# Layer 2 of a four-layer image kernel: its stores issued by Pool instead of SP, and longer transfers assumed in its list schedule

## The chip, the cores and the metric

The kernel runs on one core of one Trainium2 chip. The metric is the device time of one launch in microseconds (us), as the median of three runs; smaller is better.

The engines are called PE (matrix products), DVE (VectorE), ACT (ScalarE), POOL (GpSimd) and SP (SyncE). SP computes nothing here and issues DMAs; POOL can compute and can issue DMAs too.

## What is computed

The input x has 8 images of 32 channels with 256 x 256 pixels, in float32. Four layers follow one another, each of the form x = x + f(group_norm(x)). Layer 0 is two 3x3 convolutions in hyperbolic coordinates with batch norms, layer 1 a Laplace operator in the Fourier domain, layer 3 a local binary pattern. The change concerns layer 2, which mixes within windows of 8 x 8 pixels. Cut to what matters (`b` windows, `c` = 16, `C` = 32, `S` = 2, `WS` = 8):

```python
def _fastkan(x, ln_g, ln_b, ws, wb, bb):
    ln = _layernorm(x, ln_g, ln_b)
    basis = exp(-((ln[..., None] - GRID) / DENOM) ** 2)      # 8 grid points
    return flat(basis) @ ws.T + silu(x) @ wb.T + bb
...
y = _layernorm(wins, pn_g, pn_b)                             # over the 32 channels
a = _fastkan(y regrouped along the columns of a window, k1)  # 16 features
d = _fastkan(y regrouped along the rows of a window, k2)     # 16 features
e = _fastkan(y, k3)                                          # 32 features
z = _fastkan(a + d + e, k4)                                  # 32 features
out = z + wins
```

The result of layer 2 is x3 = x2 + out, where wins is the group norm of x2.

## The kernel before

**Layer 2 in pieces.** `mixing` (L1338) works through one image after another in units of 128 partitions x 2048 pixels (1 MB). Each image has four kinds of jobs, and intermediate results go through DRAM because each kind wants another order of the pixels:

- `image_norm` (8 jobs an image) loads a unit of x2 (tile xt), normalizes it, writes y (tile yt) and silu(y) (tile st), and stores both. The order in DRAM makes each of these two stores eight DMAs of 128 KB (`turned`, L1392).
- `down_columns` (8 jobs) loads y (one DMA) and silu(y) (16 DMAs), applies the first map and stores a (tile ot, one DMA of 1 MB).
- `along_rows` (8 jobs) loads y and silu(y) (two DMAs each), transposes on PE, applies the second map, and stores d (tile ot, two DMAs of 512 KB).
- `third` loads y (four DMAs) and silu(y), a and d (eight DMAs each) and leaves a + d + e in the tile at. `fourth` (8 jobs of each an image) loads x2 again (tile xt), applies the last map, adds, takes the statistics for the next group norm, and stores x3 (tile xt, one DMA of 1 MB).

A map consists of `normed` (L1213, L1237: center, square, norm on PE, ACT and DVE), `front` (L1250: exponents on ACT) and `back` (L1276: products on PE; L1294: exponents on ACT; L1304: the steps from one grid point to the next on DVE). `silu` has L1328 and L1335 on DVE and L1330 on ACT. `evacuate` (L1441) brings the results from PSUM to a tile.

**What sets the order.** Nothing is ordered by hand. Every job adds tasks to a `Plan` (L120 on): an engine, an assumed duration, the buffers it reads and writes, and a `lag`, the time after the engine is free again until the result counts as there. `Plan.issue` runs a list schedule in assumed time: each engine takes the ready task of lowest rank whose buffers are free, and the instructions are written out in the order in which this schedule starts them. On the chip each engine executes its own list strictly in order and waits at semaphores. The assumed times so decide the order, and nothing else.

**The DMAs of layer 2.** All of them are issued by SP, through two helpers: `load` (L1380) plans 0.55 us for each DMA and a lag of LOAD = 10 us; `store` (L1383) plans 0.55 us for each DMA and a lag of STORE = 8 us. In the profile L1381 is any load and L1384 any store. Tiles yt, st and xt have two buffers each, shared by loads and by results that are stored; ot has one buffer (B_OT) for a and d together. A load of y, silu(y), a or d of an image waits until the stores that wrote it have landed.

In the compiled program the DMAs of a queue take eight completion semaphores in turn. A DMA that takes a semaphore waits until the one that had it before, eight DMAs earlier on its queue, has landed.

**What else touches POOL and SP.** Once an image, the statistics of x3 are turned into a group norm (`combine_stats`), whose power of -0.5 is computed by POOL (L240, L241) between two DVE operations (L239, L259). In layer 0 the third pass stores its 64 units from POOL (L810), with 1.0 us and a lag of 16 us planned for each.

Of the kernel before, what the change touches and what calls it, by code (L numbers as in the profile page):

```python
# [1337 lines left out]
def mixing(cx, x2, norms, x3, ydr, sdr, adr, ddr):  # L1338
# [3 lines left out]
    nc = cx.nc  # L1342
    out_norms = cx.stat.tile([P, NB, 2], F32, name="norm3", tag="norm3")
    nc.scalar.preload_act_table_set(LOG_SET)
    with (
# [27 lines left out]
        plan = Plan()  # L1373
# [1 line left out]
        unit = lambda pool, tag, bufs, late=0.0: Buf(pool, [P, UN], tag, bufs, late)  # L1375
        half = lambda h: slice(h * HF, (h + 1) * HF)
        mem = {(n, b): Buf(None, None, None, 0) for n in "ysad" for b in range(NB)}
        LOAD, STORE = 10.0, 8.0

        def load(dmas, reads, bufs):  # L1380
            plan.add("SP", 0.55 * len(dmas), lambda: [nc.sync.dma_start(o(), i) for o, i in dmas], reads, bufs, lag=LOAD)  # L1381

        def store(dmas, bufs, writes):  # L1383
            plan.add("SP", 0.55 * len(dmas), lambda: [nc.sync.dma_start(o, i()) for o, i in dmas], bufs, writes, lag=STORE)  # L1384

        def by_row(dr, k):

# [20 lines left out]
        def image_norm(b, k):  # L1408
            if k == 0:

                scaled[b] = Buf(work, [P, NC], "cs", 2)
                plan.add(
                    "DVE", 0.2,
                    lambda: nc.vector.tensor_scalar(scaled[b][:], center[32][:], norms[:, b, 0:1], None, ALU.mult),
                    [], [scaled[b]],
                )
            xin = x2[b].rearrange("c (rb r) w -> rb c (r w)", rb=4)
            xt = unit(io, "xt", 2)
            load([(lambda: xt[:], xin[:, :, k * UN : (k + 1) * UN])], [], [xt])
            y, sg = unit(io, "yt", 2, L_Y), unit(io, "st", 2, L_Y)  # L1420
            xs = mixer.normed(xt, scaled[b], 32, vecs[:, 2, b : b + 1], mixer.spread)
            plan.add(
                "DVE", 1.25,
                lambda: nc.vector.tensor_scalar(
                    y[:], xs[:].rearrange("p i n -> p (i n)"), pn[:, 0:1], pn[:, 1:2], ALU.mult, ALU.add
                ),
                [xs], [y],
            )
            put = lambda dr, name, t: store(
                [(i, lambda o=o: o(t)) for o, i in turned(dr[b], k)], [t], [(mem[name, b], k)]  # L1430
            )
            put(ydr, "y", y)
            mixer.silu(y, sg)
            put(sdr, "s", sg)
# [10 lines left out]
        def down_columns(b, hf, k):  # L1445
            ch = hf * 16
            at = lambda dr: dr[b][:, ch : ch + 16, k * UN : (k + 1) * UN].rearrange("h c q -> c h q")
            y, sg = unit(io, "yt", 2), unit(io, "st", 2)
            load([(lambda: y[:], at(ydr))], [mem["y", b]], [y])

            dmas = []
            for j in range(4):
                for i in range(4):
                    src = sdr[b][:, ch + 4 * i : ch + 4 * i + 4, k * UN + j * FD : k * UN + (j + 1) * FD]
                    dmas.append(
                        (lambda i=i, j=j: sg[32 * j : 32 * j + 32, i * FD : (i + 1) * FD], src.rearrange("h c q -> c h q"))
                    )
            load(dmas, [mem["s", b]], [sg])
            es = mixer.front(kans[1], y)
            acc = mixer.back(kans[1], es, sg)  # L1460
            out = unit(io, "ot", B_OT)
            evacuate(acc, out, kans[1].bias)
            store([(at(adr), lambda: out[:])], [out], [(mem["a", b], (hf, k))])

        def along_rows(b, k):
# [54 lines left out]
            for g in range(2):  # L1520
                pd = mixer.two(L_D)
                plan.add("PE", 1.2, lambda pd=pd, g=g: turn_back(pd, g), [dc], [pd])
                for c in range(2):
                    for s in range(2):
                        plan.add(
                            "DVE", 0.4, lambda pd=pd, g=g, c=c, s=s: ordered(pd, g, c, s), [pd], [(ot, (g, c, s))]
                        )
            dst = ddr[b].rearrange("h (c s) q -> s (h c) q", s=2)
            store(
                [(dst[s][:, k * n : (k + 1) * n], lambda s=s: ot[:, s, :]) for s in range(2)],  # L1530
                [ot], [(mem["d", b], k)],
# [190 lines left out]
def layers(ctx: ExitStack, tc: tile.TileContext, ins, out):  # L1722
# [26 lines left out]
    x3 = image("x3_", [P, NPIX])  # L1749
    rows = [8, NC, 32 * W]  # L1750
    norms = mixing(cx, x2, norms, x3, *(image(n, rows) for n in ("y_", "s_", "a_", "d_")))

    tc.strict_bb_all_engine_barrier()
# [120 lines left out]
```

## Time and profile before

| | us |
|---|---|
| median of three runs | 14024.65 |
| lowest, highest | 14023.85, 14066.98 |
| the profiled execution, its own time | 14021.73 |
| its span in the profile | 14020.0 |
| busy: PE, DVE, ACT, POOL in the whole span | 10705.7, 8731.4, 7714.0, 166.6 |
| layer 2 within the span | 5715 to 12815 |
| an image of layer 2 in its middle part | 856 to 864 |

The mean granted clock of PE is 0.842 of full speed. The profile is one execution. In its views, "L1276" is a line of the kernel, "acc<-en" says that tile acc is written from tile en, and "SPq" is SP's queue of DMA issues. A line of the waits view reads: engine and line that waited, who ended the wait, then us in total, number of waits, longest. "DMA yt<-y" as the one who ended a wait is a transfer that landed. The DMA queues of the profile are q1 for all that SP issues and q0 for what POOL issues.

### The profile page before, as it was taken

The numbers are of one execution on the slowest core, as the hardware profiler recorded it, in microseconds if no ns is written. First come the engines' busy times: TensorE is split into PE (matmuls) and PEld (weight loads), VectorE is DVE, ScalarE is ACT, GpSimd is POOL, SyncE is SP. The second block draws the span as 40 slices with busy tenths as digits, with TensorE's granted clock in tenths as the row PEclk, the third lists the DMA queues.
The fourth block names the chain that finished last, engine by engine and source line by source line (L and its number), as shares of the span: only waits on it lengthen the run. The fifth ranks groups of instructions, "written<-read, shape, count | busy, mean of one in ns | idle before, by whom it ended". The sixth has DMA issues, their size and how long they took to land.

```text
span 14020.0 us, 359842 instructions
## 1 busy us (share of the span) xinstructions
PE 10705.7 (76%) x165700; PEld 4220.3 (30%) x165700; DVE 8731.4 (62%) x7524; ACT 7714.0 (55%) x6456; POOL 166.6 (1%) x340
## 2 busy tenths in 40 slices
PE   5877899974447899367887878878788788987666
PEld 1222233320016566122332323323232233322222
DVE  3544343344564554256787878878787788887555
ACT  2332444443310222366877778777777778775555
POOL 0000000000000000100000000000000000000000
PEclk8887889975557899588998989989899899998777
DMA  5344333345642244455566556655665565553444
GB/s 95 75 91 91 95 100 103 102 116 187 196 148 77 95 149 149 109 148 144 143 150 155 145 145 150 153 147 137 156 150 151 141 151 147 132 132 98 129 126 126
DMA packets 1562774, 1834.96 MB, mean 131 GB/s; under 512 B 634352, under 2 KB 1279536, under 8 KB 1495728
## 3 DMA queue, kind: packets, MB, share of 16 engines
q1 hardware_dynamic: 1527472, 1744.72, 47.9%
q0 software_dynamic: 33792, 67.21, 1.5%
q8 instruction: 1301, 21.32, 0.6%
q14 instruction: 209, 1.71, 0.0%
HBM read 1140.39 MB, written 671.12 MB: 129 GB/s over the span
## 4 chain that ended last, share of the span: by engine, by line
PE 15%; DVE 14%; DMA 11%; ACT 10%; SPq 5%; issue 4%; DVEq 0%; ACTq 0%; POOL 0%; POOLq 0%
PE acc L1276 10%; DVE en L1304 8%; DMA raw<-x 4%; ACT e L1250 4%; DMA yt<-y 3%; DMA xt<-x 3%; SPq L1381 2%; DVE xc L1237 2%; PE q L1196 2%; SPq L1701 1%; DVE s L1682 1%; ACT e L1294 1%; ACT xc L1213 1%; PE q L1221 1%; SPq L1384 1%
## 5 line engine op out<-in xcount | busy, mean ns | idle before, releaser
L1276 PE MATMUL acc<-en,k_kw 32*32 32x512 f32 x49152 | 2164.5, 626 | 492.1 <-DVE en L1304 454.3
L1304 DVE SCALAR_TENSOR_TENSOR en<-e,en 128x2048 f32<-128x2048 f32 x1024 | 2343.7, 2289 | 210.6 <-PE acc L1276 155.7
L1250 ACT ACTIVATE e<-xc,off 128x2048 f32<-128x2048 f32 x768 | 1515.0, 2008 | 569.2 <-DVE xc L1237 489.2
L1304 DVE SCALAR_TENSOR_TENSOR en<-e 128x2048 f32<-128x2048 f32 x512 | 1170.8, 2287 | 348.4 <-ACT e L1294 190.8
L1276 PEld LDWEIGHTS acc<-en,k_kw 32*32 32x32 f32 x49152 | 710.4, 105 | 1482.9 <-DVE en L1304 1009.7
L1276 PE MATMUL acc<-e,k_kw 32*32 32x512 f32 x16384 | 1036.2, 673 | 104.0 <-ACT e L1294 35.5
L1237 DVE TENSOR_TENSOR xc<-xc,q 128x1024 f32<-128x1024 f32 x640 | 751.0, 1215 | 489.8 <-PE q L1230 489.5
L1294 ACT ACTIVATE e<-e 128x2048 f32<-128x2048 f32 x512 | 970.3, 1924 | 1.5
L1682 DVE TENSOR_TENSOR s<-raw 128x2313 f32<-128x2313 f32 (+2 forms) x256 | 627.7, 2495 | 478.3 <-DMA raw<-x 478.3
L1668 PE MATMUL acc<-s,mats 32*32 32x512 f32 x16384 | 697.9, 728 | 231.9 <-ACT s L1685 223.1
L1685 ACT ACTIVATE s<-s,vecs 128x2313 f32<-128x2313 f32 (+2 forms) x256 | 554.4, 2170 | 553.7 <-DVE s L1682 553.7
L405 ACT ACTIVATE u<-acc,k_vec 128x1024 f32<-128x1024 f32 x256 | 270.8, 1108 | 1062.3 <-DMA v<-u 694.0
L391 PE MATMUL acc<-pad,wb 32*32 32x512 f32 x18432 | 736.9, 649 | 141.1 <-issue 131.8
L1213 ACT ACTIVATE lsq<-q 128x1024 f32<-128x1024 f32 x512 | 526.6, 1028 | 530.6 <-PE q L1196 468.1
L434 DVE TENSOR_TENSOR u<-u,q 128x1024 f32<-128x1024 f32 x256 | 312.4, 1220 | 738.6 <-PE q L429 547.7
L391 PE MATMUL acc<-pad,k_cw 32*32 32x512 f32 x18432 | 736.6, 625 | 15.7 <-ACT u L405 10.8
L711 PE MATMUL n<-sq,k_gather 128*32 128x512 f32 x1024 | 243.7, 1045 | 439.6 <-ACT sq L729 438.2
L1276 PE MATMUL acc<-sg,k_kws 128*32 128x512 f32 x4096 | 504.5, 636 | 47.9 <-DVE sg L1335 40.6
L1196 PE MATMUL q<-yt,k_center 32*32 32x512 f32 x4096 | 313.2, 722 | 284.3 <-DMA yt<-y 227.8
L1213 ACT ACTIVATE xc<-q 128x1024 f32<-128x1024 f32 x512 | 529.3, 1034 | 0.0
L348 PE MATMUL q<-f,k_spread 32*128 32x512 f32 x1024 | 392.8, 853 | 173.2 <-DVE pad L588 93.0
L1071 PE MATMUL po<-ea,us 128*128 128x256 f32 x2048 | 506.5, 391 | 1.2 <-ACT us L1067 1.2
(291 smaller groups left out, 15967.4 us busy)
## 6 DMA issues: line engine op xcount, KB each, us to landing
v<-u SPq DMA_DIRECT2D x512, 256.0 KB
xt<-x SPq DMA_DIRECT2D x128, 1024.0 KB
pad<-v SPq DMA_DIRECT2D x64, 1024.0 KB
v<-v SPq DMA_DIRECT2D x64, 1024.0 KB
xt<-in_x SPq DMA_DIRECT2D x64, 1024.0 KB
x<-xt POOLq DMA_DIRECT2D x64, 1024.0 KB, 38.8
xt<-x SPq DMA_DIRECT2D x32, 2048.0 KB
x<-xt SPq DMA_DIRECT2D x32, 2048.0 KB
```

What stands on the lines that cost most here:

```text
L391: nc.tensor.matmul(acc[i // 2][32 * j : 32 * j + 32, i % 2, :], w[rows, tap, :], pad[rows, r : r + 2, dx : dx + W], start=tap == 0, stop=t ...
L1071: nc.tensor.matmul(po[:, t, :], us[:, c, t:W:2], ex[:, j, c, :], start=c == 0, stop=c == 1)
L1196: nc.tensor.matmul(pc[32 * j : 32 * j + 32, t, :], center[rows, :], src[rows, j * FD : (j + 1) * FD], start=True, stop=True,)
L1213: lambda pc=pc, h=h, fn=fn, out=out: nc.scalar.activation(half(out, h), flat(pc.get()), fn, bias=bias),
L1237: lambda pr=pr, h=h: nc.vector.tensor_tensor(half(xc, h), half(xc, h), flat(pr.get()), ALU.mult),
L1250: nc.scalar.activation(es[d][:], xs[:].rearrange("p i n -> p (i n)"), AF.Exp if exp else AF.Square, bias=kan.off[:, d : d + 1], scale=2.0 ...
L1276: nc.tensor.matmul(acc[bank][32 * to : 32 * to + 32, :], w[rows, out] if w.shape[-1] == P else w[rows, :], rhs[rows, cols] if rhs.shape[-1 ...
L1294: plan.add("ACT", 1.91, lambda: nc.scalar.activation(es[d][:], es[d][:], AF.Exp, scale=-1.0), [], [es[d]])
L1304: lambda: nc.vector.scalar_tensor_tensor(n[:], es[-1][:], BIG, prev[:], ALU.min, ALU.mult),
L1668: nc.tensor.matmul(acc[i][32 * j : 32 * j + 32, :], mats[part, m, part], rhs[part, 2 * j : 2 * j + 2, :], start=m == 0, stop=m == len(weig ...
L1682: nc.vector.tensor_tensor(d, raw[:, r0 + dy : R + 1 + dy, c0 + dx : c1 + dx], raw[:, r0 : R + 1, c0:c1], ALU.subtract)
L1685: nc.scalar.activation(d, d, AF.Sigmoid, scale=vecs[:, 0, b : b + 1])
```

## The change

In `mixing`, the helper `store` plans its task on POOL instead of SP, with 1.0 instead of 0.55 us for each DMA, and issues with `nc.gpsimd.dma_start`. The assumed lags become 12 us for loads and 14 us for stores. Every store of layer 2 goes through this helper: 1280 DMAs. Loads stay on SP with 0.55 us each.

```diff
-        LOAD, STORE = 10.0, 8.0
+        LOAD, STORE = 12.0, 14.0
 
         def load(dmas, reads, bufs):
             plan.add("SP", 0.55 * len(dmas), lambda: [nc.sync.dma_start(o(), i) for o, i in dmas], reads, bufs, lag=LOAD)
 
         def store(dmas, bufs, writes):
-            plan.add("SP", 0.55 * len(dmas), lambda: [nc.sync.dma_start(o, i()) for o, i in dmas], bufs, writes, lag=STORE)
+            plan.add("POOL", 1.0 * len(dmas), lambda: [nc.gpsimd.dma_start(o, i()) for o, i in dmas], bufs, writes, lag=STORE)
```

Since the schedule is computed from these numbers, the order of the instructions of layer 2 changes on all engines, from its first image on. Their number and kind stay the same but for the issuer of the stores. On POOL, the group norm of an image comes behind the last store of x3 of that image.

## The prediction

> **What bounds the kernel now.** I first read the windows view, to place layer 2. It fills 5715 to 12815 us of the 14020.0 us span. After its start-up this is its row (columns: stretch, length, busy time of PE, PE weight load, DVE, ACT, POOL, then granted clock, DMA share, GB/s):
>
> ```profile
> 5945.00:12815.00 6870.00, 5566.01 (x96336) 2034.88 (x96336) 5330.06 (x3674) 5178.19 (x4402) 6.25 (x23) 0.91 0.58 144
> ```
>
> PE is busy 81% of it, DVE 78%, ACT 75%, POOL not at all. No engine is full: the order of the work and the waits at its joints set the pace, and PE stands idle 1304 us. So the next view is who ends PE's waits in that stretch (total us, times, longest):
>
> ```profile
> PE q L1196 <- DMA yt<-y: 192.5, 32, 17.8
> PE q L1196 <- DMA xt<-x: 77.9, 5, 18.4
> PE q L1483 <- DMA yt<-y: 17.5, 2, 14.2
> PE q L1483 <- DMA st<-s: 3.0, 1, 3.0
> ```
>
> Late loads cost PE 290.9 us directly; no compute engine waits there for a store to any amount. The loads come from SP, in order, between the stores. So I read SP's own waits over the layer; L1384 are stores, L1381 loads:
>
> ```profile
> SPq L1381 <- PE q L1196: 806.6, 70, 35.0
> SPq L1384 <- DVE ot L1518: 579.8, 37, 26.5
> SPq L1384 <- DVE xt L1568: 406.2, 47, 38.9
> SPq L1384 <- DMA xt<-x: 223.5, 29, 11.9
> ```
>
> All lines at L1384 add to 1643 us, those at L1381 to 1884 us: for 1643 us SP stands before a store whose data isn't there, or whose completion semaphore is still in use, and each load behind it stands too. The timeline of SP shows how that looks (start, us, queue, line, transfer):
>
> ```profile
> 5746.67 16.66 SPq L1384 DMA_DIRECT2D y<-yt  x8
> 5763.42 0.55 SPq L1381 DMA_DIRECT2D xt<-x  x1
> 5764.07 17.10 SPq L1384 DMA_DIRECT2D s<-st  x8
> 5781.26 5.07 SPq L1384 DMA_DIRECT2D y<-yt  x8
> 5786.43 0.55 SPq L1381 DMA_DIRECT2D xt<-x  x1
> ...
> 8507.54 22.19 SPq L1384 DMA_DIRECT2D y<-yt  x8
> 8529.82 5.79 SPq L1381 DMA_DIRECT2D at<-a  x8
> ```
>
> Eight stores need 5.07 us of issue when nothing holds them, and 16 to 22 us when they stand behind a slow xt load: in the compiled program the DMAs of a queue take eight completion semaphores in turn, so each waits for the eighth before it. In the start-up (one image's norm units, 5715 to 5935 us) the xt loads come 23.6 us apart: (5904.83 - 5763.42) / 6.
>
> The only POOL stores of this kernel stand in layer 0, at L810 (min/median/max; 1 MB each):
>
> ```profile
> L810 POOL DMA_DIRECT2D x<-xt x64: 680/680/887, 3122.7 to 4083.9; - x64
> ...
> DMA to landing us min/median/max: 15.1/38.8/48.4
> ```
>
> **What the Trainium skill says.** "DMA: Bandwidth & Descriptors", section "Issuing engines are not separate DMA queues": transfers from several issuers run on the same 16 engines, and a second issuer saves only sequencer time. That fits what I expect to win, which is SP's time and not bandwidth. The same page, "Queues, rings and completion order": each DMA engine goes round its queues packet by packet, so POOL's stores would no longer stand behind an xt load in one queue. Nothing in layer 2 shows it yet, since only SP's queue carries data there. The same page, "Why a DMA increments its semaphore by 16 and not by 1": a transfer is spread over the largest number up to 16 that divides the slowest dimension of both sides. With 4 row blocks the xt load gets 4 engines; the trace agrees, with a DMA share of 0.25 from 5720 to 5745 us, when only xt loads run. POOL's L810 stores have the same shape, and the last of them ran at a share of 0.25 too (4090 to 4097 us). Layer 2's stores have slowest dimensions of 32, 16 or 128 and would get all 16. "SBUF - State Buffer", "SBUF: two separate sides": a fast-mode DVE operation on one fp32 SBUF source locks POOL out of writing DMA descriptors. Such are L1424 and L1328 (1.34 and 1.22 us against 2.29 us for two sources); no run here shows the lock.
>
> **Part 1: what SP loses.** By medians, SP's stores cost 512 x 0.601 + 512 x 0.598 + 128 x 0.378 + 64 x 0.564 + 64 x 0.344 = 720 us of issue, and 1643 us of waits. SP isn't full, so this is no saving in itself; it is worth what the loads behind gain. Of SP's waits 1643 / (1643 + 1884) = 47% belong to stores; the others wait for a buffer that PE still reads, or for semaphores of other loads, and stay. I take the same share of PE's waits: 0.47 x 291 = -137 us. The ends: 0, if the buffers are what makes these loads late, and -291.
>
> **Part 2: what POOL gains.** POOL issues 1280 DMAs; at L810's 0.68 us that is 870 us in 7100 on an idle engine. It counts only by how long eight stores take from the first issue to the last landing; call it B. The L810 landings are no direct measure, since 1 MB on four engines at the 77 GB/s seen at the end (4090 to 4100 us) takes 13.6 of the 15.1 us, leaving 1.5 us fixed. Eight stores of 128 KB: 5.5 us of issue, or 1 MB at layer 2's 144 GB/s = 7.3 us, whichever is longer, then those 1.5 us: 9 us with nothing in the way. The upper end is 27 us, half way between L810's 15.1 and 38.8, which came with loads in the way. I take 11 us, near the lower end, because a running xt load is in the way on only four of the sixteen engines. The planner now assumes 8 x 1.0 + 14 = 22 us for such a group, so its order leaves room for that. Against this, SP's groups took 5 to 22 us of issue alone, so the buffers yt, st and ot are held no longer than now.
>
> **Part 3: start-up.** A norm unit stores y and s, two groups of eight in series over eight semaphores: 2B = 22 us, beside an xt load (10 to 19 us) and ACT's 10 us. 22 replaces 23.6: 8 x -1.6 = -13 us; ends -46 (17.8 us a unit, the xt load's usual time) and +243 (B = 27).
>
> **Part 4: POOL's other work.** Once an image the group norm (L240, L241) is on POOL and DVE waits for it; it is now behind stores, and behind DVE wait PE and ACT. Today's waits are 5.8 us in 8 times. Each can be between 0.7 and B = 11 us; I take 3: 8 x 3 - 5.8 = +18 us; ends 0 and +82. The DVE lock touches single operations of 1.3 us; I take nothing, since POOL's groups are a few us in an otherwise free 50.
>
> **Part 5: the new delays, 12 and 14 for 10 and 8.** They cost no instruction; they reorder every engine of layer 2. An order with longer loads puts other work before their readers, which is the kind of wait listed above; an order with longer stores delays the users of a buffer. No row prices this. I take 0 and keep 1% of the layer, 70 us, either way as my choice; four steady images lie 856 to 864 us apart, so a worse order would repeat seven times.
>
> **Sum.** -137 - 13 + 18 = -132 us. The profiled execution took 14021.73 us around its span of 14020.0, 2.9 us below the median of 14024.65; so 14024.65 - 132 = 13893 us.
>
> **Rivals.**
> 1. Stores land late (slower). One mechanism: groups of eight on POOL's eight semaphores, each waiting for the last. It decides above B = 23.6 / 2 = 11.8 us: from there the start-up grows by 16 x (B - 11.8), and yt and st, two buffers each, stay taken, so loads come no earlier. With B = 27: +243, and nothing from part 1: 14024.65 + 243 = 14268 us. For it: the median landing of 38.8 us at L810. Against: the shape on four engines. Chance 0.28.
> 2. The change does not reach the bound. The 860 us an image are set by the chain PE to DVE (PE L1276 waits 454.3 us for DVE en L1304), and a load that is earlier only turns into that wait. Parts 3 and 4 remain: 14024.65 - 13 + 18 = 14030 us, no change. Chance 0.15.
> 3. All load waits go, start-up at 17.8 us: 14024.65 - 291 - 46 = 13688 us. For it: loads and SP are 18% of the chain in layer 2. Chance 0.09.
> The forecast, 13780 to 13980 us: 0.48.
>
> **Numbers.** About 0.3%, 42 us, is what a measurement of this kernel can tell from no change. Faster: 0.48 + 0.09 = 0.57; same 0.15; slower 0.28. The range goes from 13730 to 14230 us: it leaves out half of rival 1 and most of rival 3.
>
> **What would show it.** Part 1: L1384 gone from SP's waits, PE's waits for yt and xt near 150 us. Part 2: POOL's L1384 at 0.7 us each, landings near 11 us for a group; over 12 us, with waits of DVE or ACT for y<-yt, s<-st or a<-ot, speak for rival 1. Part 3: xt loads 22 us apart. Part 4: DVE L259 waiting 2 to 4 us an image. Rival 2: the DMA waits shrink, images stay 860 us apart. I am wrong if images come further apart with POOL's stores on time: then the order of part 5 is the cause.

## The result and the profile after

The kernel after takes 13885.28 us in the median (13881.95 to 13906.22), the kernel before in the same series 14024.25 us: a ratio of 0.9898, 95% interval 0.9876 to 0.992. That is 139 us less; 132 had been forecast. The profiled execution of the kernel after, the slowest of its four, has a span of 13904.0 us, which is 116 less than in the profile before, at a mean granted clock of 0.85.

Three instants divide layer 2 in both traces: its first xt load, its first load of y (here the start-up ends), and the group norm at the end of each image.

| us from the first xt load of layer 2 | before | after |
|---|---|---|
| first load of y | 219.7 | 161.7 |
| first group norm | 1749.8 | 1655.8 |
| second to fifth | 2610.5, 3466.5, 4327.2, 5190.8 | 2501.2, 3342.1, 4190.8, 5038.2 |
| last group norm | 7097.4 | 6952.6 |
| where the first xt load stands in the span | 5714.9 | 5740.0 |

The layer is 145 us shorter: 58 of them are gone by the end of the start-up, 87 come later, in images that are 841 to 849 us apart in the middle instead of 856 to 864. Against this the layer begins 25 us later in this profile, though nothing ahead of it was changed; I come back to that at the end.

The windows view of the kernel after from its start-up to its last group norm (columns as in the prediction):

```profile
5900.00:12700.00 6800.00, 5587.54 (x96368) 2045.69 (x96368) 5335.00 (x3686) 5185.51 (x4405) 683.26 (x1192) 0.92 0.57 146
```

PE, DVE and ACT do the work they did before in 70 us less; POOL is busy with 683 us of issue, and the DMA share did not rise. PE's own busy time did not fall (5587.54 us, before 5566.01), so the slightly higher granted clock is not what gained. Who ends PE's waits for loads once the first y has come, from 5945 us on in both traces (to 12700 here, to 12815 in the prediction's list):

```profile
PE q L1196 <- DMA yt<-y: 102.3, 28, 10.0
PE q L1196 <- DMA xt<-x: 26.6, 5, 5.9
PE q L1483 <- DMA yt<-y: 19.7, 1, 19.7
PE acc L1276 <- DMA st<-s: 2.6, 3, 1.7
```

Together 151 us, where it was 291. SP's own waits over layer 2:

```profile
SPq L1381 <- PE q L1196: 1474.0, 84, 37.3
SPq L1381 <- PE acc L1276: 641.9, 83, 31.4
SPq L1381 <- DMA xt<-x: 312.9, 34, 15.4
SPq L1381 <- DMA x<-xt: 308.1, 27, 40.7
SPq L1381 <- PE q L1483: 280.3, 31, 18.2
```

L1384 is gone from SP, as it had to be. But SP is no freer: its waits at L1381 add to 3738 us, where loads and stores together had 1880 + 1546 = 3427 us in nearly the same stretch. SP now stands mostly before loads whose buffer PE still reads (L1196, L1276). The time it no longer spends in front of stores it spends waiting for buffers.

POOL's stores, one line of the kernel, with the work that POOL waited for and those that waited for POOL:

```profile
L1384 POOL DMA_DIRECT2D y<-yt x512: 522/582/1729, 5772.4 to 11308.9; - x171
L1384 POOL DMA_DIRECT2D s<-st x512: 522/607/1307, 5787.1 to 11322.2; - x171
...
  DVE ot L1518: 2299.8, 64
  DVE xt L1568: 1482.8, 66
  ACT ot L1441: 1006.5, 45
...
  ACT st L1330: 27.0, 5
  DVE st L1328: 10.1, 2
  DVE yt L1424: 2.4, 3
...
DMA to landing us min/median/max: 2.6/5.4/13.7
```

An issue of y or s takes 0.58 to 0.61 us, a store lands 5.4 us after its issue began in the median, and compute engines wait for stores 40 us in the whole layer, where it was 130 in the kernel before, nearly all of it in the start-up. POOL itself stands 4.8 ms, by the three lines in the middle, before data that isn't there yet. Nothing is queued behind it, so that costs nothing.

In the start-up the chain of waits shows what paces it now (start, us, what):

```profile
5787.08 7.40 DMA s<-st
5794.52 0.53 issue
5795.05 9.32 DMA y<-yt
5804.41 0.53 issue
5804.94 1.06 POOL s L1384 x2
5806.05 11.05 DMA s<-st
```

A store lands 7.4 to 11.1 us after its issue, mostly about 9.5, and the next one on its semaphore goes. The xt loads are no longer in this chain. The 9.5 us are one turn of a semaphore, from one store to the next that takes it, and not the prediction's B, which runs from the first issue of eight to the last landing. POOL's timeline shows one whole group, the eight y stores from 5795.05 us on, and the s stores that take their semaphores (in brackets: idle before, and who ended it):

```profile
5795.05 0.53 POOL L1384 DMA_DIRECT2D y<-yt  x1 [2.38 <-DMA s<-st]
...
5803.55 0.52 POOL L1384 DMA_DIRECT2D y<-yt  x1 [0.88 <-DMA s<-st]
5804.94 1.64 POOL L1384 DMA_DIRECT2D s<-st  x3 [0.86 <-DMA y<-yt]
...
5813.08 1.31 POOL L1384 DMA_DIRECT2D s<-st  x1 [0.62 <-DMA y<-yt]
```

The eighth s store waits for the eighth y store, which lands shortly before 5813.08: B is 18 us here. But the groups are not in series. The first s goes at 5804.94, as soon as the first y has landed, so the groups follow one another at 9.5 to 10 us. By the updates of the semaphores in the trace, B is 14 to 18 us for the groups of the start-up until the last few, and 10 to 11 us in the median later.

### The profile page after: what moved, and what is told of

Its sections match the earlier page's. It is cut to its first block, busy times and chain, and to the rows that moved or that the text cites. A ratio compares the mean times of both kernels' runs of the same rounds, so it can differ in the third digit from the quotient of the medians.

```text
span 13904.0 us, 360826 instructions
## 1 busy us (share of the span) xinstructions
PE 10721.7 (77%) x165700; PEld 4228.4 (30%) x165700; DVE 8730.9 (63%) x7524; ACT 7715.9 (55%) x6456; POOL 910.6 (7%) x1620
## 4 chain that ended last, share of the span: by engine, by line
PE 14%; DVE 13%; DMA 11%; ACT 9%; issue 8%; SPq 3%; POOL 0%; DVEq 0%; ACTq 0%; POOLq 0%
PE acc L1276 9%; DVE en L1304 7%; DMA raw<-x 4%; ACT e L1250 3%; DMA yt<-y 2%; DVE xc L1237 2%; SPq L1701 1%; PE q L1196 1%; DMA xt<-x 1%; DVE s L1682 1%; ACT st L1330 1%; DMA st<-s 1%; SPq L1381 1%; PE q L1230 1%; PE q L1221 1%
## 5 line engine op out<-in xcount | busy, mean ns | idle before, releaser
L1276 PE MATMUL acc<-en,k_kw 32*32 32x512 f32 x49152 | 2154.8, 620 | 459.6 <-DVE en L1304 428.1
L1276 PEld LDWEIGHTS acc<-en,k_kw 32*32 32x32 f32 x49152 | 713.3, 104 | 1447.5 <-DVE en L1304 961.6
L1276 PE MATMUL acc<-e,k_kw 32*32 32x512 f32 x16384 | 1043.0, 662 | 109.3 <-ACT e L1294 33.7
L391 PE MATMUL acc<-pad,k_cw 32*32 32x512 f32 x18432 | 736.7, 625 | 16.8 <-ACT u L405 11.4
L1276 PE MATMUL acc<-sg,k_kws 128*32 128x512 f32 x4096 | 507.4, 638 | 64.8 <-DVE sg L1335 51.9
L1221 PE MATMUL q<-lsq,k_gather 128*32 128x512 f32 x2560 | 460.8, 658 | 86.4 <-ACT xc L1213 85.7
```

The lines of the kernel that those rows point to most:

```text
L391: nc.tensor.matmul(acc[i // 2][32 * j : 32 * j + 32, i % 2, :], w[rows, tap, :], pad[rows, r : r + 2, dx : dx + W], start=tap == 0, stop=t ...
L1221: nc.tensor.matmul(pn[32 * i : 32 * i + 32, 0, :], gather[:], sq[:, i, :], start=True, stop=True)
L1276: nc.tensor.matmul(acc[bank][32 * to : 32 * to + 32, :], w[rows, out] if w.shape[-1] == P else w[rows, :], rhs[rows, cols] if rhs.shape[-1 ...
```

## The experiments

All ratios are to the kernel before, with 95% intervals. Diffs are against the kernel before unless another is named. The kernels differ in three things that the change made together: who issues the stores, the order of the work, and the lags that lead to that order.

**The queue alone (e1).** The plan stays as it was, so all compute engines keep their order; only the issuer changes.

```diff
-            plan.add("SP", ..., lambda: [nc.sync.dma_start(o, i()) for o, i in dmas], ...)
+            plan.add("SP", ..., lambda: [nc.gpsimd.dma_start(o, i()) for o, i in dmas], ...)
```

> The plan is that of the kernel before (store tasks on SP, 0.55 us for each DMA, lags of 10 and 8 us), so every compute engine keeps the order of before; only the issue of the layer-2 stores goes through Pool. Theory 1 (loads no longer stand behind stores on SP; the new lags are worth nothing): nearly all of the gain, about 13895 us, ratio 0.99; start-up 162 us instead of 220. Theory 2 (the new order is what gains): within 0.3% of before, 14010 to 14040 us.

Measured: 0.9932 (0.9918 to 0.9945), two thirds of the gain. Layer 2 takes 7005.6 us, 92 less: 42 by the end of the start-up (178.2 us, not the 162 expected), 50 later.

**The order alone (e2).** The plan of the kernel after, with POOL as planned engine and lags of 12 and 14, but `nc.sync` in the issue.

> The plan is that of the changed kernel (store tasks on Pool, 1.0 us for each DMA, lags of 12 and 14 us), so every compute engine keeps its order; the stores are issued by SP, in the places where that plan starts them. Theory 1: no gain, or a loss, since the order reckons with loads that do not stand behind stores: 14020 to 14120 us. Theory 2: about 13900 us.

Measured: 0.9979 (0.9968 to 0.9991), between the two theories. The new order is worth 0.2% with all stores still on SP.

**POOL with the old lags (e3).** The kernel after with `LOAD, STORE = 10.0, 8.0`.

> The changed kernel with the old lags of 10 and 8 us; stores are planned and issued on Pool. Theory 1: as the changed kernel within 0.3%, 13850 to 13930 us. Theory 2: near before, 13990 us or more.

Measured: 0.9925 (0.9913 to 0.9938). Of the 1.02% of the change, 0.75% stay without its lags.

**The lags alone (e4).** The kernel before with `LOAD, STORE = 12.0, 14.0`.

> The kernel before with the lags of 12 and 14 us; stores are planned and issued on SP. Theory 1: as before within 0.3%, since SP still holds loads behind stores. Theory 2: a good part of the gain, 13960 us or less.

Measured: 0.9974 (0.9964 to 0.9984). So the queue alone is worth 0.7% and the lags alone about 0.25%, and the two about add up: 0.9932 x 0.9974 = 0.9906, beside 0.9898 (0.9876 to 0.992) measured for both.

**Which lag (e10, e11).** The kernel after with `LOAD, STORE = 12.0, 8.0`, and with `10.0, 14.0`.

> The kernel after with the load lag of 12 and the store lag put back to 8. The kernel after is at 0.9898, and with both lags put back at 0.9925. If the load lag carries the 0.26% (loads placed earlier in SP's queue), this run gives about 0.990; if the store lag carries it (the planner reads y and s back later behind their stores), about 0.9925.

> The kernel after with the store lag of 14 and the load lag put back to 10: the other half of the same question. If the load lag carries the gain, about 0.9925; if the store lag does, about 0.990; if the two only work together, both this run and the one with the load lag alone stay near 0.9925.

Measured: 0.9911 (0.9898 to 0.9925) and 0.9907 (0.9893 to 0.9921). Both lie between the two expected values, and their intervals touch or overlap those of both neighbours. It isn't decided; that each lag carries half fits, and so does noise.

**Which stores (e5, e6).** Only the groups of eight (y and s) on POOL, and then only a, d and x3, with the plan of before. Both are one condition in `store`:

```diff
-            ... [nc.sync.dma_start(o, i()) for o, i in dmas] ...
+            ... [(nc.gpsimd if len(dmas) == 8 else nc.sync).dma_start(o, i()) for o, i in dmas] ...
```

> Order of before on every compute engine. Only the stores of y and silu(y), the groups of eight DMAs, are issued by Pool; a, d and x3 stay on SP. Theory A (what costs is that groups of eight share SP's eight semaphores with slow loads, so the group and all behind it stand): most of the 0.68% that moving all stores gave under this order, ratio 0.994 or less. Theory B (what costs is SP standing before a store whose data is not there, above all ot and xt, 1310 us of SP waits): only the start-up gains its 40 us, ratio 0.997.

> Order of before on every compute engine. Only the stores of a, d and x3 are issued by Pool; y and silu(y) stay on SP in their groups of eight. Theory A: within 0.2% of before, start-up as before (220 us). Theory B: about half a per cent faster, start-up as before.

Measured: 0.9933 (0.992 to 0.9946) for y and s, the whole effect of the queue; 1.0012 (1.0006 to 1.0019) for a, d and x3, a small loss. These are SP's waits for stores in the kernel that keeps y and s on SP:

```profile
SPq L1384 <- DMA xt<-x: 212.7, 23, 13.5
SPq L1384 <- DVE yt L1424: 163.2, 33, 14.9
SPq L1384 <- DMA yt<-y: 70.9, 78, 2.7
```

All its L1384 waits add to 504 us, 1042 less than before, since `DVE ot L1518`, `DVE xt L1568` and `ACT ot L1441` are no longer among them. And the kernel is not faster. A thousand microseconds of SP standing before unfinished results could go without any gain. They moved: SP's waits at L1381 rise from 1880 to 2724 us, most of it before buffers that PE still reads (L1196, L1276 and L1483, 1211 us before, 1911 now), and PE's own waits for loads are no shorter (322 us from 5970 us on, after its first y, where the kernel before had 291). What cost must lie with the y and s stores: their standing behind an xt load, or SP's time to issue 1024 of them, 614 us by the medians. The experiments on the split tell these two apart.

**What an xt load does to the stores behind it** can be read from the trace of the kernel before, at the s stores of 5764.07 us (the timeline is in the prediction). The load ahead of them goes at 5763.42 and lands at 5780.60. SP issues seven stores until 5770; the eighth takes the semaphore of the load and goes at 5780.62. But the seven don't land earlier either. By the updates of their semaphores the first one lands at 5780.84, 16.8 us after its issue, where the y stores from 5781.26 on, with no load ahead of them, take 2.4 us each. While the seven are in flight, the DMA share (last column but one) sinks close to the 0.25 of the load alone:

```profile
5764.00:5769.00 5.00, 1.90 (x10) 0.52 (x8) 0.00 (x0) 4.51 (x4) 0.00 (x0) 0.50 0.87 190
5769.00:5780.00 11.00, 6.65 (x44) 0.83 (x40) 5.81 (x4) 7.01 (x7) 0.00 (x0) 0.50 0.30 91
```

So most engines are through with the stores by 5769, and what is left of the stores moves when the load is done. In the kernel after, POOL issues an s store at 5787.08, 0.4 us after SP issued an xt load that lands at 5804.56, and the store lands in 7.4 us (first line of the chain above). From the other queue it no longer stands behind the load.

**The slow load itself (e7).** If that load is the cause, the stores may stay where they are. Each xt load of layer 2 becomes four DMAs of one row block each. It is planned as one DMA of 0.55 us, so that no order moves; the inserted lines put the later ones six further down.

```diff
+        def load_four(t, src):
+            plan.add(
+                "SP", 0.55, lambda: [nc.sync.dma_start(t[32 * j : 32 * j + 32], src[j]) for j in range(4)],
+                [], [t], lag=LOAD,
+            )
+
...
-            load([(lambda: xt[:], xin[:, :, k * UN : (k + 1) * UN])], [], [xt])
+            load_four(xt, xin[:, :, k * UN : (k + 1) * UN])
```

The second xt load, in `fourth`, is edited alike.

> The kernel before, with each load of xt in layer 2 issued as four DMAs of 32 partitions by SP (planned as one, so the order of every engine stays). If the load is slow because four row blocks put it on four DMA engines, it lands in about 5 us instead of 16 to 20, the store groups behind it are not held, the start-up falls from 220 to some 150 us, and the whole gains about 1%: 13900 us. If the load is slow for another reason, nothing gains, and SP only has 384 more DMAs to issue: 14020 us or more.

Measured: 0.9796 (0.9782 to 0.9809), twice the gain expected and twice that of the change, with all stores on SP. The start-up takes 136.1 us. SP's timeline in it (start, us, queue, line, transfer):

```profile
5753.53 1.70 SPq L1388 DMA_DIRECT2D xt<-x  x4
5755.33 5.42 SPq L1384 DMA_DIRECT2D s<-st  x8
5760.85 5.08 SPq L1384 DMA_DIRECT2D y<-yt  x8
5767.27 1.70 SPq L1388 DMA_DIRECT2D xt<-x  x4
```

No group takes 16 us any more, and the units follow at 13.7 us instead of 23.6. A part of a load lands 5.2 us after its issue in the median of the layer, by the updates of the semaphores; the whole load took 18.2. The windows view (columns as before) shows that the start-up is now filled with transfers, at a DMA share of 0.94; in the kernel before it was 0.54, from 5780 to 5900 us:

```profile
5780.00:5840.00 60.00, 36.25 (x215) 5.77 (x200) 31.79 (x24) 47.41 (x41) 0.00 (x0) 0.50 0.94 228
```

PE's waits for loads over the layer (`raw<-x`, L1674, is already layer 3):

```profile
PE q L1196 <- DMA yt<-y: 101.7, 16, 17.4
PE acc L1674 <- DMA raw<-x: 23.5, 7, 8.1
PE q L1196 <- DMA xt<-x: 14.8, 3, 13.3
```

Before, the same stretch, start-up included, had 227.8 us for yt and 103.2 for xt. SP's waits at L1384 stay at 1479 us in this faster kernel (before: 1546), which says the same as the experiment on a, d and x3. What did go is what waited for an xt load, stores (223.5 us before) and loads (209.9 us before) alike:

```profile
SPq L1384 <- DMA xt<-x: 18.3, 34, 1.4
SPq L1381 <- DMA xt<-x: 10.7, 21, 0.8
```

The split gains 2.0%, the move of the stores 0.7%. So the load held up more than the stores: later loads stood behind it as well, and PE waited for it itself. How the rest of the gain divides between these wasn't measured.

**The split and the change together, and the split with the lags alone (e8, e9).** The same edit on the kernel after; and the same edit with lags of 12 and 14 but stores on SP.

> The changed kernel with each load of xt in layer 2 as four DMAs of 32 partitions (planned as one). PE's waits for xt (84 us in the changed kernel's profile) fall to about 20 us; the start-up stays near 160 us if its pace is set by the store groups on Pool. 13820 us, ratio to before 0.985. If loads are late because their buffers are, no change against the changed kernel: ratio 0.990.

> The kernel before with layer 2's image loads split into four DMAs by row block, as in e7, and the two lags of the kernel after (12 and 14); stores stay on SP. The same split on the kernel after gave 0.9781, and on the kernel before 0.9796. If the small rest between those two is the lags alone, with the store queue worth nothing once no slow load sits among SP's eight completion semaphores, this run gives 0.976 to 0.978. If the lags were worth something only while the load was slow, it gives 0.9796 or more, and the rest in e8 belongs to the store queue.

Measured: 0.9781 (0.9768 to 0.9794), more than expected, with a start-up of 140.6 us and not 160, and 0.9776 (0.9763 to 0.979). Once no slow load stands in SP's queue, these runs show no difference between stores issued by SP and by POOL. So it was not SP's time of issue that the move had gained. What the two have over the plain split, 0.15 to 0.2%, is of the size of the lags, with intervals that overlap.

**The same fault elsewhere (e12).** Layer 0's third pass moves its image by the same pattern: L787 loads from SP, L810 stores from POOL. On the kernel after with the split, both are split by row block too, planned as before.

```diff
-... nc.sync.dma_start(xt[:], xin[:, :, cols(k)]) ...
+... [nc.sync.dma_start(xt[32 * j : 32 * j + 32], xin[j, :, cols(k)]) for j in range(4)] ...
-... nc.gpsimd.dma_start(xout[:, :, cols(k)], xt[:]) ...
+... [nc.gpsimd.dma_start(xout[j, :, cols(k)], xt[32 * j : 32 * j + 32]) for j in range(4)] ...
```

> The kernel after with layer 2's image loads split by row block, as in e8 (0.9781), and in layer 0's third pass each image load and each store split into four DMAs in the same way, planned at the same cost as before, so that no order moves. If that pass waits for such transfers as layer 2 did, some tens of microseconds go: 0.974 to 0.977. If it waits for VectorE and not for its transfers, it stays at 0.978; and if four times as many stores on POOL hold the work behind them, it is above 0.978.

Measured: 13391.39 us, 0.9531 (0.9518 to 0.9544), the fastest version, with a far larger gain than expected. Layer 2 now begins at 5374.9 us, 346 earlier than with the split in layer 2 alone. L810 in this kernel (min/median/max in ns, first and last start, then the time to landing), where each store has a quarter of the size; in the kernel before it was 680 ns an issue, 38.8 us to landing in the median, and the last store at 4083.9:

```profile
L810 POOL DMA_DIRECT2D x<-xt x256: 489/492/673, 3105.7 to 3752.3; - x128
...
DMA to landing us min/median/max: 2.8/8.5/13.0
```

And the windows of 500 us in the middle of that pass, before and in this kernel:

```profile
3150.00:3650.00 500.00, 230.92 (x752) 43.84 (x748) 249.62 (x296) 200.54 (x121) 21.89 (x36) 0.50 0.58 187
```

```profile
3150.00:3650.00 500.00, 341.55 (x1112) 65.30 (x1104) 380.50 (x452) 299.19 (x179) 91.23 (x191) 0.51 0.91 286
```

With every engine half idle and the DMA share at 0.58, the pass looked bound by nothing. Its DMAs were bound, each on four of sixteen engines; the share goes to 0.91, and everything runs 1.5 times as fast. Which of the two splits did it, load or store, wasn't tried.

## Why the prediction was right, point by point

The number was right, 13893 for 13885 us, but its terms were not; their errors cancel, so that it came so close is luck.

| step | forecast, us | measured, us |
|---|---|---|
| 1: the load waits of the steady stretch | -137 | -50 (queue alone), -87 (with the lags) |
| 3: the start-up | -13 | -42 (queue alone), -58 (with the lags) |
| 4: the group norm behind stores | +18 | 0 |
| 5: the new lags | 0 | -37 (0.26% by the experiment on the lags) |
| sum | -132 | -129; the kernel after -139 |

- **Part 1** failed in size, as a term for the queue. With the queue alone PE's waits for loads fell from 292 to 252 us (5945 to 12600 us), and the time after the start-up by 50 us, not 137. The step that failed is the share of 47%: SP's waits of a thousand microseconds for ot and xt weigh in it, and taken away they gained nothing; the time rose by 0.12%. A queue that waits is no loss while the loads behind it would wait for a buffer anyway, and the trace of the kernel after shows just that (1474 us before `PE q L1196`). Without the 1085 us for ot and xt results the share would have been 23%, or 67 us. The sign named for this part, PE's waits near 150 us, did come, with 151 in the kernel after. But it came with the lags: in the same stretch it is 263 with POOL and the old lags, 227 with the new load lag alone and 175 with the new store lag alone (single profiles). And 140 us less of waiting went with only 87 us less of time.
- **Part 2** had the issue about right, 0.6 us for 0.68. Its B of 11 us is near the median of the whole layer, but in the start-up, where part 3 uses it, B was about 18 us, far above the 11.8 us from which the first rival was to decide. The start-up got shorter all the same, because the groups overlap. The reading of L810 was off too: the 77 GB/s are the mean of a stretch that runs on after the transfer had ended. From 4090 to 4097 us it is 99 GB/s, which leaves 4.5 us fixed and not 1.5.
- **Part 3** had the right sign, from a wrong form. By its own sum, two groups in series of 18 us each, the start-up would have grown by about 100 us. What paces it is a turn of a semaphore: two turns of 9.5 us are 19 us a unit, and eight units save 8 x 4.6 = 37 us. That is near the 42 us of the queue alone. The 58 us of the kernel after lie outside the end of 46 that the prediction gave; there the new order also puts the first load of y ahead of ten stores of s that stood before it. Nor did the xt loads come 22 us apart: the last eight of the start-up come 13.3 us apart, since they no longer wait for stores.
- **Part 4** did not come: DVE waits for the group norm as long as before (us, times).

```profile
  POOL norm L241: 6.0, 8
```

- **Part 5** was set to nothing for want of a row. It is a gain of about 0.25%: 0.26% by the lags alone and 0.21% by the order alone, both clear of 1; between 0.9925 and 0.9898 with POOL, and between 0.9796 and 0.9776 with the split, the intervals overlap. It lies within the 70 us allowed.
- **Rival 1**, stores that land late: they did in the start-up, by the prediction's own B, but the loss did not follow. The start-up is 58 us shorter, and compute engines wait for stores 40 us where it was 130. **Rival 2** is refuted by images 841 to 849 us apart. **Rival 3** did not come: 151 of 291 us of waits are still there, and it takes the split load to remove most of them (92 us are left with it, from 5945 to 12600 us, layer 3's loads not counted).

Two statements of the Trainium skill bear on this. "DMA: Bandwidth & Descriptors", "Issuing engines are not separate DMA queues", says that a second issuer saves only the sequencer's time. Here it gained 0.7%, and not by that time: with the load split, stores on SP and on POOL gave the same time. It took the y and s stores out of a queue in which a slow load went before them. The same page, "Why a DMA increments its semaphore by 16 and not by 1", gives the number of engines of a transfer as the largest up to 16 that divides the slowest dimension of both sides. The prediction has that rule, but only to judge what an xt load leaves free for the stores. It was the larger lever, and the trace agrees: a share of 0.25 while the whole load runs alone, and 0.94 in the start-up, stores included, with the load in four parts.

What stays open. In the kernel before, an xt load held up the stores behind it in two ways: SP waited for the semaphore that it held, and stores already issued landed only after it. How the gain of the queue divides between the two is not known: moving the stores and splitting the load each remove both. Nor is it known why layer 2 begins at 5728.8 to 5757.9 us in seven of the eight profiles with stores on POOL (5721.3 in the other, the split on the kernel after) and at 5712.7 to 5727.4 us in those with all stores on SP. The code ahead of it is the same, and these are single profiles.

## What to carry to other kernels

Before moving DMAs to another queue, look for the one slow transfer that the queue stands behind: a landing time far above its neighbours' of the same size, or a DMA share of a quarter where it runs alone, points to a slowest dimension that uses few of the sixteen engines. Mending it gained three times as much as moving the stores away from it (2.0% for 0.7%), left nothing for the move to gain, and brought another 2.5% in a pass that looked idle. And a queue's total of waits is no measure of what it costs; count only those waits whose end something behind is really late for.

## What was not expected of the hardware

- POOL's y and s stores went out in packets of 4096 bytes, the same rows from SP in packets of 1024 (131072 of them). No run separates the two for speed alone; with the load split, both issuers gave the same time.
- DVE operations of the kind for which the prediction named a lock against POOL took 1.34 us (L1424) and 1.22 us (L1328) in the median before and after. POOL's longest issue of y was 1.73 us against 0.58 in the median. If there is a lock, it costs nothing that this case shows.
- Smaller DMAs were issued faster: four of 256 KB took SP 1.70 us, 0.43 us each, where one xt load of 1 MB took 0.55; at L810 they took POOL 0.49 us each, where one of 1 MB took 0.68.
